# Three delays of 0.8 made 1.3 ahead of the weight products in an eight-pass graph kernel

## The chip, the cores and the metric

The kernel runs on one core of a Trainium2 chip. The metric is the device time of one execution in microseconds (us). A core has five engines that run side by side, each through its own queue in program order: TensorE (PE, matrix products; PEld are its weight loads), VectorE (DVE), ScalarE (ACT), GpSimd (POOL) and SyncE (SP, which here issues the loads from memory). An engine that needs another's result waits for a semaphore.

## The reference, cut to what matters

A graph of 3327 nodes with 64 features each has one adjacency matrix `adj`. Four residual layers follow one another, each on the layer norm of `x` cut at zero. Written out by its products with a 3327 x 3327 matrix, the work is eight passes:

```python
h = relu(layernorm(x))
# layer 0: two gated cells, each with m = adj @ h             -> passes 0, 1
# layer 1: w @ h, w = weights by rank among the non-zeros     -> pass 2
# layer 2, with w = adj * adj, three hops:                    -> passes 3, 4, 5
for W, b in ((W0, b0), (W1, b1), (W2, b2)):
    h = w @ h
    h = h @ W.T + b
# layer 3, two hops:                                          -> passes 6, 7
for k in range(2):
    agg = adj @ h
    h = tanh(concatenate([agg, h], axis=1) @ W[k])
x = x + h
```

"Pass k" below is the kernel's own index `k`. Pass 3 is the first hop of layer 2; passes 6 and 7 are the two hops of layer 3.

## The kernel before, in words

**Tiling.** The nodes are padded to 26 blocks of 128 and split into two halves of 13. Four chunks of blocks (`CH`, L52) hold 3, 3, 3 and 4 blocks of each half: chunks 0, 1 and 2 are 384 columns wide, chunk 3 is 512. Chunks 0 and 1 are group 0, chunks 2 and 3 are group 1. A tile is 128 source nodes against all the target columns of a group. In pass 7 chunk 1 is split in two: chunk 4 (256 columns) and chunk 5 (128 columns).

**Units.** A unit `(k, c, t)` adds to the sums of pass k and chunk c what tile t gives: in all passes but pass 2 four matmul instructions at L607 (two for each half of the nodes, since the type is f32). 26 units finish the sums of a chunk. `alone` and `joint` (L639, L655) write the list of units once; at the end of a stage the last 6 or 8 tiles are gone through for one chunk and then for the other, so that one chunk's sums are ready while TensorE works on the other's. `run` (L711) goes through the list and issues it.

**What happens between the units.** When a chunk's sums are complete, `propagate` calls `begin(c, after[k](...))` (L613). The `after_k` functions are generators: they issue a few instructions and then `yield` a number of microseconds. `spend(us)` (L374) is called after every unit with that unit's estimated TensorE time, 0.86 x width / 512 (L611, `STREAM_US`): 0.645 for 384 columns, 0.86 for 512, 0.43 for 256 and 0.215 for 128. It takes that from every waiting generator's number, and one that reaches zero or less goes on at once, ahead of the next unit. So a `yield` sets after how many units the next instructions stand in the queues. What is left over from a wait isn't carried to the next. At the end of the list the remaining generators are finished in order (L1045).

**After pass 3** (`after_3`, L973): `evacuate` (L750) copies the sums from PSUM into a work tile, with ScalarE (L753) for chunks 1 and 3 and VectorE (L755) for 0 and 2; then `yield`; then `dense_to_nodes` (L759) issues 4 products per block through `mm` (L307) on TensorE; then `yield 0.8`; then VectorE adds the bias (L980).

**After passes 6 and 7** (`after_6`, L999; `after_7`, L1011): `evacuate_stacked` (L823) copies one half of the sums with ScalarE (L824) and the other with VectorE (L825) into `both[c]`; then `yield`; then `stacked_to_nodes` (L767) issues the products with the weights, 8 instructions per block, the first 4 of a block with the half that ScalarE copied and the next 4 with VectorE's (L774); then ScalarE's tanh. In pass 6 a `yield 8.0` and transposes on VectorE follow (L803); in pass 7 a `yield 0.8`, the addition to x on VectorE (L1019) and the DMA of the output, which ScalarE's queue issues (L1021).

**PSUM.** Eight banks of 512 columns: four for sums, four for the rest, handed out by `take` and given back by `give` (L316, L329), first in, first out. In pass 7 chunk 5 takes two banks for its sums, one for each half (L585).

**Squares.** Passes 3 to 5 need the squares of the tiles. `prepare` (L444) squares a tile some units ahead, and `square` (L438) gives it to ScalarE (L440), or, where `(t.q + c) % 3` is 0 and no generator of a chunk is under way, to VectorE (L442).

Of the kernel before, what the change touches and what calls it, by code (L numbers as in the profile page):

```python
# [96 lines left out]
def kernel(  # L97
# [198 lines left out]
    def blocks(c):  # L296
        return CH[c][1] - CH[c][0]
# [31 lines left out]
    def give(i):  # L329
        released[i] = max(released) + 1  # L330
        (idle_sums if i < 4 else idle_temps).append(i)

    def nodes(c):

        return feat.tile([P, blocks(c), 2, D], F32, name=f"y{c}")

    def flat(t):
        return t.rearrange("p b s d -> p b (s d)")

    def groups(t):  # L340
        return t.rearrange("p b s d -> p (b s) d")

    def xchunk(c):
        return xs[:, CH[c][0]:CH[c][1]]
# [405 lines left out]
    def evacuate(acc, c, busy=False):  # L750
        m = work.tile([P, CWM], F32, name="t2")[:, :width(c)]
        if c % 2 or busy:
            nc.scalar.copy(m, acc[0][1][:, :width(c)])  # L753
        else:
            nc.vector.tensor_copy(m, acc[0][1][:, :width(c)])  # L755
        give(acc[0][0])
        return m

    def dense_to_nodes(ft, w, c):  # L759

        i, ps = take()
        v = view(ps, c)
        for b in range(blocks(c)):
            mm(v[:, b, :], ft[:, b * P:(b + 1) * P], bd[:, w - WL1, :])
        return i, v

    def stacked_to_nodes(c, w):  # L767

        i, ps = take()
        v = view(ps, c)  # L770
        for b in range(blocks(c)):
            for s in range(2):
                for n in range(2):
                    nc.tensor.matmul(v[upper(n), b, upper(s)], both[c][:, s, b * P + n * D:b * P + (n + 1) * D], w(s),  # L774
                                     start=True, stop=True)
        return i, v
# [19 lines left out]
    def transpose_on_vector(h, c):  # L796

        for s in range(2):
            to = both[c][:, s].rearrange("p (b q n) -> p b q n", q=4, n=32)
            for q in range(4):  # L800
                for f in range(2):
                    at = (1 - s) * D + f * 32
                    nc.vector.transpose(to[at:at + 32, :, q], h[q * 32:(q + 1) * 32, :, s, f * 32:(f + 1) * 32])  # L803
                if q % 2:
                    yield 1.5
# [17 lines left out]
    def evacuate_stacked(acc, c):  # L823
        nc.scalar.copy(both[c][upper(0), 0], acc[0][1][upper(0), :width(c)])  # L824
        nc.vector.tensor_copy(both[c][upper(1), 1], acc[1][1][upper(1), :width(c)])  # L825
        for i in {acc[0][0], acc[1][0]}:
            give(i)
# [144 lines left out]

    def after_3(c, acc):  # L973
        m = evacuate(acc, c)
        yield 0.8
        v = dense_to_nodes(m, WL2, c)
        yield 0.8
        yk = nodes(c)
        n = 2 * blocks(c)
        nc.vector.tensor_tensor(groups(yk), v[1].rearrange("p b (s d) -> p (b s) d", d=D),  # L980
                                brow[:, 0:1, :].to_broadcast([P, n, D]), ALU.add)
        give(v[0])
        y[4][c] = yk
# [15 lines left out]

    def after_6(c, acc):  # L1000
        evacuate_stacked(acc, c)
        yield 0.8
        v = stacked_to_nodes(c, lambda s: w3[:, 0, s])
        yk = nodes(c)
        nc.scalar.activation(flat(yk), v[1], AF.Tanh)
        give(v[0])
        y[7][c] = yk
        yield 8.0
        yield from transpose_on_vector(yk, c)

    def after_7(c, acc):  # L1011
        evacuate_stacked(acc, c)
        yield 0.8
        v = stacked_to_nodes(c, lambda s: w3[:, 1, s])
        t = work.tile([P, 4, 2, D], F32, name="t2")[:, :blocks(c)]
        nc.scalar.activation(flat(t), v[1], AF.Tanh)
        give(v[0])
        yield 0.8
        nc.vector.tensor_tensor(flat(xchunk(c)), flat(xchunk(c)), flat(t), ALU.add)  # L1019
        g0, g1 = CH[c]  # L1020
        nc.scalar.dma_start(out=out[:, g0:g1], in_=xs[:, g0:g1])  # L1021

    after[:] = [after_0, after_1, after_2, after_3, after_4, after_5, after_6, after_7]


# [60 lines left out]
```

## Time and profile before

| | |
|---|---|
| device time, three runs | 708.05, 708.03, 707.58 us, median 708.03 |
| the profiled execution's own time | 707.41 us |
| its span, first to last instruction | 705.5 us, at 0.999 of TensorE's full clock |
| TensorE busy | 680.6 us (96%) |
| VectorE busy / ScalarE busy | 351.7 us (50%) / 271.3 us (38%) |
| loads of the adjacency matrix | 199.46 MB on SP's queue, 76.1% of 16 DMA engines' span |

The times of one profiled execution are in us from the start of the span. In lines of the timeline the columns are start, length, engine, line, operation, tiles, shapes and count; in brackets stands the idle time of the engine before it, and what ended it. Matmuls overlap, so a line's length includes the last one's way through the array. The first slices up to about 80 us are passes 0 and 1 with the constants, the stretch to about 335 us is mostly pass 2, then come passes 3 to 5 up to about 560 us, and passes 6 and 7 to the end.

### The profile page before, as it was taken

What the parts mean: (1) busy time and instruction counts of PE and PEld (TensorE: products, weight loads), DVE (VectorE), ACT (ScalarE), POOL (GpSimd) and SP (SyncE); (2) the same over time, 40 slices, a digit from 0 to 9 for tenths busy, and PEclk for the clock granted to TensorE, in tenths of its full rate; (3) what the DMA queues carried; (4) which work ended last, traced back from release to release, by engine and by line L of the source; (5) the groups of instructions that cost most, each with busy time, mean ns of one, the idle gap of its engine ahead of it and who ended that gap; (6) DMA issues with size and microseconds to landing.
All of it is one profiled execution on the core that took longest, in us unless ns stands there. A gap on an engine that the chain in (4) does not pass through costs nothing.

```text
span 705.5 us, 12624 instructions
## 1 busy us (share of the span) xinstructions
PE 680.6 (96%) x5100; PEld 362.5 (51%) x5100; DVE 351.7 (50%) x747; ACT 271.3 (38%) x421; POOL 75.7 (11%) x114
## 2 busy tenths in 40 slices
PE   1999999999999999999999999999999999999997
PEld 1454666643545787677444444333344444344464
DVE  7566835633997889847533105425271565005101
ACT  1014100212136888888997206832166500000101
POOL 4300000002291233111100000000000000000000
PEclk9999999999999999999999999999999999999999
DMA  9999996089688952683799649963997399917991
GB/s 337 401 387 404 405 406 239 1 337 384 204 284 299 313 176 83 241 296 103 266 369 354 242 163 408 405 262 112 392 366 271 105 397 405 407 64 282 403 402 36
DMA packets 68549, 201.31 MB, mean 285 GB/s; under 512 B 7228, under 2 KB 8228, under 8 KB 68492
## 3 DMA queue, kind: packets, MB, share of 16 engines
q1 hardware_dynamic: 65596, 199.46, 76.1%
q8 instruction: 40, 0.66, 0.4%
q10 hardware_dynamic: 720, 0.85, 0.3%
q0 software_dynamic: 2176, 0.20, 0.2%
q14 instruction: 17, 0.14, 0.1%
HBM read 199.45 MB, written 0.85 MB: 284 GB/s over the span
## 4 chain that ended last, share of the span: by engine, by line
PE 84%; DVE 9%; ACT 4%; issue 1%; DMA 1%; SPq 0%; ACTq 0%; DVEq 0%
PE sum L607 70%; PE temp L307 5%; ACT adj L440 4%; DVE adj L466 3%; PE temp L542 2%; PE temp L876 2%; PE sum L307 1%; PE temp L774 1%; PE sum L876 1%; DVE e L521 1%; DMA bd<-in_weights 1%; DVE both L825 1%; DVE adj L901 1%; DVE st L842 0%; DVE t L836 0%
## 5 line engine op out<-in xcount | busy, mean ns | idle before, releaser
L607 PE MATMUL sum<-adj,y 128*64 128x384 f32 (+3 forms) x3016 | 533.6, 501 | 0.8 <-DVE y L849 0.6
L607 PEld LDWEIGHTS sum<-adj,y 128*64 128x64 f32 x3016 | 233.7, 137 | 246.3 <-issue 220.9
L440 ACT ACTIVATE adj<-adj 128x768 f32<-128x768 f32 (+1 forms) x175 | 143.6, 892 | 47.3 <-PE sum L607 24.6
L466 DVE TENSOR_SCALAR adj<-adj 128x768 bf16<-128x768 f32 (+3 forms) x208 | 114.7, 599 | 39.1 <-PE temp L542 31.1
L824 ACT COPY both<-sum 64x384 f32<-64x384 f32 (+3 forms) x17 | 8.1, 478 | 196.4 <-PE sum L607 196.3
L607 PE MATMUL sum<-e,both 128*64 128x384 bf16 (+1 forms) x624 | 78.4, 339 | 0.5 <-DVE e L521 0.4
L523 ACT ACTIVATE e<-temp,bitsb 128x384 int16<-128x384 f32 (+1 forms) x117 | 66.1, 606 | 15.0 <-PE temp L307 9.9
L825 DVE COPY both<-sum 64x384 f32<-64x384 f32 (+3 forms) x17 | 9.7, 568 | 113.6 <-ACT both L824 112.4
L442 DVE TENSOR_TENSOR adj<-adj 128x768 f32<-128x768 f32 (+1 forms) x33 | 31.5, 1003 | 52.2 <-DMA adj<-in_adjT 33.4
L307 PE MATMUL temp<-adj,tri 128*64 128x384 bf16 (+1 forms) x332 | 56.8, 341 | 0.5 <-DVE e L521 0.2
L845 POOL TENSOR_TENSOR st<-st,mhalf 128x6 f32<-128x6 f32 (+1 forms) x16 | 24.5, 1529 | 288.9 <-DVE st L843 288.9
L607 PEld LDWEIGHTS <-both 128*64 128x64 bf16 x624 | 46.5, 110 | 15.5 <-issue 2.2
L307 PEld LDWEIGHTS <-tri 128*64 128x64 bf16 x416 | 33.4, 110 | 15.3 <-issue 7.4
L521 DVE TENSOR_SCALAR e<-temp 128x384 int16<-128x384 f32 (+1 forms) x49 | 30.1, 617 | 21.1 <-ACT e L523 10.5
L471 POOL DMA_DIRECT2D adj<-totals x52 | 32.7, 630 | 51.5 <-PE temp L307 42.9
L803 DVE STREAM_TRANSPOSE both<-y 32x96 f32<-32x96 f32 (+1 forms) x128 | 35.6, 278 | 2.9
L542 PE MATMUL temp<-adj,behind 128*64 128x384 bf16 x208 | 30.3, 339 | 0.9 <-DVE adj L466 0.7
L819 DVE STREAM_TRANSPOSE y<-t 32x96 f32<-32x96 f32 (+1 forms) x64 | 17.8, 278 | 25.2 <-ACT t L810 24.3
L542 PEld LDWEIGHTS <-behind 128*64 128x64 bf16 x208 | 17.0, 110 | 17.6 <-issue 15.9
L755 DVE COPY t<-sum 128x384 f32<-128x384 f32 x6 | 3.3, 554 | 35.4 <-PE sum L607 35.4
L876 PE MATMUL temp<-both,cells 128*64 128x384 f32 (+1 forms) x68 | 17.7, 521 | 0.2 <-DVE both L825 0.2
L523 ACT ACTIVATE e<-sum,bitsb 128x384 int16<-128x384 f32 (+1 forms) x28 | 16.6, 599 | 2.5 <-PE sum L307 2.0
(132 smaller groups left out, 307.5 us busy)
## 6 DMA issues: line engine op xcount, KB each, us to landing
adj<-in_adjT SPq DMA_DIRECT2D x130, 768.0 KB, 8.5
adj<-in_adjT SPq DMA_DIRECT2D x104, 896.0 KB, 12.5
xs<-in_x SPq DMA_DIRECT2D x1, 640.0 KB
adj<-totals POOLq DMA_DIRECT2D x26, 3.0 KB, 5.3
adj<-totals POOLq DMA_DIRECT2D x26, 3.5 KB, 3.6
out<-xs ACTq DMA_DIRECT2D x2, 192.0 KB
out<-xs ACTq DMA_DIRECT2D x1, 256.0 KB
stage<-in_weights SPq DMA_DIRECT2D x2, 112.0 KB, 13.4
```

Of the source, the lines that this page charges most:

```text
L307: nc.tensor.matmul(out[hs], lhsT[:, hs], rhs, start=start, stop=stop)
L440: nc.scalar.activation(sq, v, AF.Square)
L442: nc.vector.tensor_tensor(sq, v, v, ALU.mult)
L466: nc.vector.tensor_scalar(t.mask.view[:rows, half], t.view()[:rows, half], 0.0, None, op0=ALU.not_equal)
L471: nc.gpsimd.dma_start(out=t.mask.view[P - 1:P], in_=totals[t.g][t.q:t.q + D + 1:D, :])
L521: nc.vector.tensor_scalar(wide[:, s], ps[:, :w], BITS, 0.0, op0=ALU.add, op1=ALU.max)
L523: nc.scalar.activation(wide[:, s], ps[:, :w], AF.Relu, bias=bitsb)
L542: nc.tensor.matmul(counts[c][1][s * D:(s + 1) * D, :w], behind[:, NQ - 1 - t.q:NQ - 1 - t.q + D], t.mask.view[:, s, t.cols(c)], start=firs ...
L607: nc.tensor.matmul(acc[h][1][h * D:(h + 1) * D, :w], yq[h], rhs[h], start=first and n == 0, stop=last and n == len(terms) - 1)
L803: nc.vector.transpose(to[at:at + 32, :, q], h[q * 32:(q + 1) * 32, :, s, f * 32:(f + 1) * 32])
L845: nc.gpsimd.tensor_tensor(st[:, 3, :n], st[:, 2, :n], mhalf[:, :n], ALU.pow)
L876: nc.tensor.matmul(ps[upper(1 - s), :w], cells[:, cell, s, g, :], both[c][:, s], start=True, stop=True)
```

## The change

Three numbers: the `yield` between the copy of the sums and the products with the weights, in `after_3`, `after_6` and `after_7`.

```diff
     def after_3(c, acc):
         m = evacuate(acc, c)
-        yield 0.8
+        yield 1.3
         v = dense_to_nodes(m, WL2, c)
         yield 0.8
...
     def after_6(c, acc):
         evacuate_stacked(acc, c)
-        yield 0.8
+        yield 1.3
         v = stacked_to_nodes(c, lambda s: w3[:, 0, s])
...
     def after_7(c, acc):
         evacuate_stacked(acc, c)
-        yield 0.8
+        yield 1.3
         v = stacked_to_nodes(c, lambda s: w3[:, 1, s])
```

No instruction is added or dropped. `after_5`, which has the same shape, keeps its 0.8.

## The prediction

> **What bounds the kernel now.** I read the page's first part, then the waits of TensorE, then the timeline around each of the 13 products that the edit concerns, last the chain that ended last.
>
> ```profile
> PE 680.6 (96%) x5100; PEld 362.5 (51%) x5100; DVE 351.7 (50%) x747; ACT 271.3 (38%) x421; POOL 75.7 (11%) x114
> ```
>
> TensorE bounds the kernel, so only time in which it stands still can be won. Its waits from 335 us to the end:
>
> ```profile
> PE temp L774 <- DVE both L825: 0.9, 4, 0.3
> PE temp L774 <- ACT both L824: 0.3, 1, 0.3
> PE temp L307 <- ACT t L753: 0.3, 1, 0.3
> ```
>
> With one of 0.6 us for a layer norm (L849) that is all of them: in passes 3 to 7 TensorE waits for copies of sums, and never for a DMA. The idle times understate the cost, because a matmul's modelled end covers part of the gap. I measure from start to start instead. A product block without a wait and one with it, both 24 instructions of pass 6:
>
> ```profile
> 578.71 0.87 PE L774 MATMUL temp<-w,both 128*64 128x64 f32 x24
> 579.41 3.07 PE L607 MATMUL sum<-adj,y 128*64 128x384 f32 x17
> ```
>
> ```profile
> 627.16 0.47 ACT L824 COPY both<-sum 64x384 f32<-64x384 f32 x1 [42.23 <-PE sum L607]
> 627.66 0.56 DVE L825 COPY both<-sum 64x384 f32<-64x384 f32 x1 [34.76 <-ACT both L824]
> ...
> 627.80 0.28 PE L774 MATMUL temp<-w,both 128*64 128x64 f32 x4
> ...
> 628.28 0.80 PE L774 MATMUL temp<-w,both 128*64 128x64 f32 x20 [0.19 <-DVE both L825]
> ...
> 628.91 2.32 PE L607 MATMUL sum<-adj,y 128*64 128x512 f32 x10
> ```
>
> The first takes 0.70 us to the next unit (578.71 to 579.41), the second 1.11: chunk 2 loses 0.41. The copies follow each other, ScalarE 0.22 us after the sums' last matmul (which ends 0.86, one unit, before 627.80), VectorE after ScalarE; 1.33 us after the sums the second half is there (628.27). One unit of 0.86 is too short for that, two (1.72) are enough.
>
> **What the skill says.** The Trainium skill, "PSUM — Partial Sum Buffer", section "PSUM bank collisions raise a hardware error", says that software must keep two engines apart on one bank and quadrant, readers too. The trace agrees and is stricter: VectorE's copy waits for ScalarE's although they read different partitions, except in chunk 5, whose halves lie in two banks (701.11 and 701.16). "TensorE: Matmul & The Clock Gate", section on the 16 sub-arrays, says that weight loads can be pulled ahead of running matmuls while ScalarE and VectorE are strictly first in, first out. The trace agrees: 0.14 us loads lie inside 0.32 us steps. "DMA: Bandwidth & Descriptors", section "Anatomy of one DMA", says that a DMA's semaphore wait is done on the issuing sequencer. The trace agrees: ScalarE's last tanh (702.38) stands behind an output DMA (701.94) that waits for an add.
>
> **The change part by part.** First, where each product goes. After the sums: chunks 0 and 1 of pass 3 and chunk 0 of pass 6, and chunk 3 of pass 3, are followed by 384-wide units; 2 x 0.645 = 1.29 is just short of 1.3, so 3 units instead of 2. Chunk 2 of passes 3, 6 and 7 is followed by 512-wide units: 2 instead of 1. Chunks 1 and 3 of pass 6 are followed by 384 and 512: 1.505, so 2 units before and after; they don't move. Chunk 3 of pass 7 is followed by 0.645, 0.43, 0.215 in turn: 4 units (1.935) instead of 2 (1.075). Chunk 0 of pass 7 by 0.43s: 4 instead of 2. Chunk 4 by six units of 0.215, together 1.29: it falls behind all of them, to the end. Chunk 5 is at the end anyway.
>
> Then, what each stall is worth. Unstalled, 12 products of pass 3 take 0.65 (407.36 to 408.01, 413.18 to 413.83), 16 take 0.87 (513.32 to 514.19, the like products of pass 5); of L774, 24 take 0.70 and 32 take 0.94 (636.42 to 637.36).
>
> Pass 3, chunks 0 and 1, pass 6, chunk 0: no stall, gain 0. The moved adds, tanh and transposes come one unit later; the next pass needs them ten and more units later, which hides them. Chunk 2 of pass 3: 0.67 instead of 0.65, gain 0.02.
>
> Pass 3, chunk 3:
>
> ```profile
> 364.54 0.57 ACT L753 COPY t<-sum 128x512 f32<-128x512 f32 x1
> ...
> 365.16 1.09 PE L307 MATMUL temp<-bd,t 128*64 128x128 f32 x16 [0.27 <-ACT t L753]
> ...
> 366.08 6.30 PE L607 MATMUL sum<-adj,y 128*64 128x384 f32 x38
> ```
>
> The copy is late behind ScalarE's squares. Weight loads come every 0.32, each at the start of the matmul before its own; the last two before the product, at 363.75 and 364.07, put its due time at 364.72. It starts at 365.16, and takes 0.92: 0.44 + 0.05 = 0.49 lost. A unit later it is due at 365.36, the copy is there at 365.15: gain 0.49. The unit that is pulled ahead of it needs a square that ended before the copy began (ScalarE's queue is in order), so it doesn't wait. One thing more moves: chunk 3's generator lives a unit longer, so one square (tile 20, chunk 1) goes to ScalarE (0.74 each, 24 in a row from 365.00) instead of VectorE. It would end at 368.79 and is used near 369.8; later ones have more. Cost 0, or 0.74 if that cover is gone.
>
> Pass 6, chunk 2: gain 0.41; the product is now due at 628.66, past 628.27. Pass 7, chunk 2: 656.91 to 658.08 is 1.17, gain 0.47; due at 657.77, VectorE done at 657.39.
>
> Pass 7, chunk 3:
>
> ```profile
> 664.97 0.69 DVE L825 COPY both<-sum 64x512 f32<-64x512 f32 x1 [5.60 <-ACT both L824]
> ...
> 665.16 0.28 PE L774 MATMUL temp<-w,both 128*64 128x64 f32 x4
> ...
> 665.72 1.03 PE L774 MATMUL temp<-w,both 128*64 128x64 f32 x28 [0.27 <-DVE both L825]
> ...
> 666.59 2.76 PE L607 MATMUL sum<-adj,y 128*64 128x128 f32 x24
> ```
>
> 1.43 instead of 0.94: 0.49 lost. But here another wait takes its place. The sums' banks are given back in the order chunk 2, chunk 3 of pass 6, chunk 2, chunk 3 of pass 7, and taken in that order by chunk 0, chunk 4 and twice by chunk 5. Chunk 5's second half therefore writes the very bank that VectorE is emptying until 665.66. Before, the product stood ahead of it and took the wait; now chunk 5's first unit comes at 665.16 and waits to about 665.71, between 0.44 (if two of its passes run first) and 0.55. Gain between +0.05 and -0.06; I take 0.
>
> Pass 7, the tail. Chunk 0: 696.14 to 697.25, gain 0.41 on TensorE. Now the product runs 697.00 to 697.70, and with two more units chunk 4's sums end at 698.56 (before 698.98). But tanh (697.92 to 698.41), the add (to 699.00) and the output DMA's issue (0.34, to 699.37) now all stand ahead of chunk 4's copy in the queues: the add comes two units after the product, exactly at the end of chunk 4's units. So ScalarE copies at 699.47 instead of 698.78 (before 699.20), VectorE from 699.86 to 700.29, chunk 4's product ends at 700.29 + 0.05 + 0.40 = 700.74, tanh 700.96 to 701.34, add to 701.80, DMA issue to 702.17, chunk 5's tanh at 702.27, add, last DMA issue at 702.90. Before it stood at 703.01. Gain 0.11, between -0.2 (0.05 more per hand-over, six of them) and 0.41.
>
> Loads: SP issues the last 24 of pass 7 between 636.6 and 676.9; at the 405 GB/s of the full slices 24 x 768 KB need 46.6 us, to about 683, and the last tile is used at 694. DMA doesn't take the gain.
>
> Sum: 0.02 + 0.49 + 0.41 + 0.47 + 0 + 0.11 = 1.50. The profiled execution would go from 707.41 (span 705.5 and 1.9 around it) to 705.91. It lies 0.62 under the median of the runs shown; from 708.03 I forecast 706.5.
>
> **The rivals.** *More*: chunk 5's unit isn't held by the bank (+0.49), and the tail keeps its 0.41 (+0.30): gain 2.29, 705.7. Against it: the order of the banks is fixed by the code. *Less*: the tail costs its bad end (-0.2) and one of the three stalls is only half gone (0.2): 1.50 - 0.31 - 0.2 = 1.0, 707.0. For it: the tail's hand-overs are all taken at their shortest. *Nothing*: the edit doesn't do what it says, the stalls return at the next unit, as the bank shows for chunk 3 of pass 7: 708.0. Against it: elsewhere no unit needs a bank just emptied. *Slower*: ScalarE's strict queue. If the squares have less than 0.74 us of slack at tile 20 (the chain passes through L440 from 336 to 364), the added square holds TensorE by 0.74 and chunk 3's 0.49 is not won, and in the tail the late copy costs 0.5: -(0.02 + 0.41 + 0.47) + 0.74 + 0.5 = +0.34, 708.4. It decides where TensorE would reach that unit before 368.8; I expect about 369.8.
>
> **How the numbers follow.** Forecast 0.50 (its own range 706.0 to 707.0), more 0.15, less 0.20, nothing 0.09, slower 0.06. The range takes in more and less: 705.6 to 707.4; nothing and slower, 0.15, stay out. About 0.2% (1.4 us) is what a measurement of this kernel can tell from no change. The forecast lies just beyond it: 0.35 of its 0.50 and all of "more" give faster 0.50; 0.05 of slower and some unseen wait give slower 0.06; same 0.44.
>
> **What would show it.** The products of chunk 2 (passes 6, 7) and of chunk 3 (pass 3) take 0.70 and 0.87 to the next unit, without a wait; chunk 5's first L607 waits for VectorE L825 by 0.4 to 0.6; the output DMA of chunk 0 is issued between tanh and chunk 4's copy; 25 squares stand in a row on ScalarE. I am wrong if TensorE waits for L440 near 369, or if the tail from chunk 0's last unit (695.28) to the last DMA issue is over 7.9 us.

## The result, and the profile after

| | before | after |
|---|---|---|
| device time, median of 11 runs | 708.03 us | 706.86 us |
| ratio, 95% interval | | 0.9981 (0.9973 to 0.9989) |
| profiled execution: span | 705.5 us | 703.7 us |

By the ratio the gain is 1.3 us of 708.03, between 0.8 and 1.9 (the two medians differ by 1.17); forecast were 1.5 (706.5). The interval lies wholly on the faster side, but it doesn't settle whether the gain is more or less than 0.2%.

Where in the profiled executions the time went is told by marks that both have: the start of a copy of sums. Of the 1.84 us between the spans, 0.40 had gone before the first edited place was reached (chunk 2's copy of pass 3 starts at 356.10 and 355.70). Up to there the programs are the same, so two executions differ by that much on their own. The rest, in us:

| from | to | before | after | difference | forecast |
|---|---|---|---|---|---|
| copy of chunk 2, pass 3 | copy of chunk 0, pass 3 | 50.19 | 49.67 | -0.52 | -0.51 |
| ... | copy of chunk 2, pass 6 | 220.87 | 220.88 | +0.01 | 0 |
| ... | copy of chunk 2, pass 7 | 29.16 | 28.75 | -0.41 | -0.41 |
| ... | copy of chunk 3, pass 7 | 8.04 | 7.57 | -0.47 | -0.47 |
| ... | copy of chunk 0, pass 7 | 31.14 | 31.24 | +0.10 | 0 |
| ... | issue of the last output DMA | 7.51 | 7.36 | -0.15 | -0.11 |
| together | | 346.91 | 345.47 | -1.44 | -1.50 |

The whole stretch, from the start of chunk 2's copy of pass 3 to the issue of the last output DMA, is the measure of the experiments below: all that the edit touches lies in it, and nothing of what differs at the start.

The first part of the page of the kernel after follows. The busy times are nearly those of before, and one instruction has gone from VectorE to ScalarE:

```profile
PE 679.8 (97%) x5100; PEld 372.9 (53%) x5100; DVE 350.1 (50%) x746; ACT 271.8 (39%) x422; POOL 80.0 (11%) x114
```

TensorE's waits from 335 us on (engine, line and tile, who was waited for: us in total, times, longest). The products L774 and L307 are gone from the list, and one wait is new, that of L607 for VectorE's copy (L825):

```profile
PE sum L607 <- DVE y L849: 0.6, 1, 0.6
PE sum L607 <- DVE both L825: 0.2, 1, 0.2
```

In the timeline of the kernel after at pass 6, chunk 2, VectorE's copy ends at 627.31. The 24 products begin at 627.75 and are one group; it is 0.69 us from their start to the next unit, where it was 1.11.

```profile
626.25 0.47 ACT L824 COPY both<-sum 64x384 f32<-64x384 f32 x1 [42.23 <-PE sum L607]
...
626.75 0.56 DVE L825 COPY both<-sum 64x384 f32<-64x384 f32 x1 [34.76 <-ACT both L824]
...
627.75 0.87 PE L774 MATMUL temp<-w,both 128*64 128x64 f32 x24
628.44 6.83 PE L607 MATMUL sum<-adj,y 128*64 128x512 f32 x32
```

At pass 3, chunk 3, it is 0.87 from the product to the next unit, without a wait. ScalarE's copy is as late as before, behind its squares, but the product now comes one unit later.

```profile
364.14 0.58 ACT L753 COPY t<-sum 128x512 f32<-128x512 f32 x1
...
364.94 1.04 PE L307 MATMUL temp<-bd,t 128*64 128x128 f32 x16
365.81 6.62 PE L607 MATMUL sum<-adj,y 128*64 128x384 f32 x40
```

And at pass 7, chunk 3, where the wait was forecast to move: chunk 5's first unit (128 columns) now waits for the end of VectorE's copy, and the products behind it don't. Of that unit one half of the nodes runs at once and the other waits; the weight loads (the last two lines) show the two halves 0.55 us apart, 663.38 and 663.93, far more than the 0.17 us for which TensorE stood idle.

```profile
663.18 0.69 DVE L825 COPY both<-sum 64x512 f32<-64x512 f32 x1 [4.74 <-ACT both L824]
...
663.93 1.08 PE L607 MATMUL sum<-adj,y 128*64 128x128 f32 x6 [0.17 <-DVE both L825]
664.63 1.13 PE L774 MATMUL temp<-w,both 128*64 128x64 f32 x29
...
663.38 0.14 PEld L607 LDWEIGHTS sum<-adj,y 128*64 128x64 f32 x1
663.93 0.20 PEld L607 LDWEIGHTS sum<-adj,y 128*64 128x64 f32 x4 [0.42 <-DVE both L825]
```

In the tail, ScalarE's output DMA of chunk 0 stands ahead of its copy of chunk 4. In the kernel before it did so too, but its issue ended 0.28 us before the copy began, and the copy waited for its sums:

```profile
698.58 0.34 ACTq L1021 DMA_DIRECT2D out<-xs  x1
699.20 0.37 ACT L824 COPY both<-sum 64x256 f32<-64x256 f32 x1 [1.24 <-PE sum L607]
```

In the kernel after the copy follows 0.04 us behind the DMA's issue, and what it waited for is the add (VectorE, L1019) for which that DMA waited (the last line holds the copies of chunks 4 and 5 together):

```profile
696.23 0.49 ACT L1016 ACTIVATE t<-temp 128x384 f32<-128x384 f32 x1 [1.95 <-PE temp L774]
697.35 0.34 ACTq L1021 DMA_DIRECT2D out<-xs  x1
697.73 0.76 ACT L824 COPY both<-sum 64x256 f32<-64x256 f32 x2 [1.00 <-DVE xs L1019]
```

### The profile page after: what moved, and what is told of

Its sections match the earlier page's. It is cut to its first block, busy times and chain, and to the rows that moved or that the text cites. A ratio compares the mean times of both kernels' runs of the same rounds, so it can differ in the third digit from the quotient of the medians.

```text
span 703.7 us, 12628 instructions
## 1 busy us (share of the span) xinstructions
PE 679.8 (97%) x5100; PEld 372.9 (53%) x5100; DVE 350.1 (50%) x746; ACT 271.8 (39%) x422; POOL 80.0 (11%) x114
## 4 chain that ended last, share of the span: by engine, by line
PE 91%; DVE 7%; issue 0%; ACT 0%; DMA 0%; POOL 0%; ACTq 0%; DVEq 0%; POOLq 0%
PE sum L607 77%; PE temp L307 5%; PE temp L542 2%; PE temp L876 2%; PE sum L307 1%; DVE adj L466 1%; PE temp L774 1%; PE sum L876 1%; DVE e L521 1%; DVE st L842 1%; DVE adj L901 1%; DVE t L836 1%; DVE y L841 0%; DVE st L834 0%; DMA xs<-in_x 0%
## 5 line engine op out<-in xcount | busy, mean ns | idle before, releaser
L607 PE MATMUL sum<-adj,y 128*64 128x384 f32 (+3 forms) x3016 | 534.5, 502 | 0.7 <-DVE y L849 0.6
L607 PEld LDWEIGHTS sum<-adj,y 128*64 128x64 f32 x3016 | 243.5, 137 | 237.3 <-issue 212.4
L440 ACT ACTIVATE adj<-adj 128x768 f32<-128x768 f32 (+1 forms) x176 | 144.2, 893 | 45.8 <-PE sum L607 21.9
L607 PE MATMUL sum<-e,both 128*64 128x384 bf16 (+1 forms) x624 | 78.5, 339 | 0.5 <-DVE e L521 0.5
L825 DVE COPY both<-sum 64x384 f32<-64x384 f32 (+3 forms) x17 | 9.6, 569 | 110.5 <-ACT both L824 110.5
L307 PE MATMUL temp<-adj,tri 128*64 128x384 bf16 (+1 forms) x332 | 56.8, 341 | 0.5 <-DVE e L521 0.2
L607 PEld LDWEIGHTS <-both 128*64 128x64 bf16 x624 | 46.6, 110 | 15.5 <-issue 2.2
L307 PEld LDWEIGHTS <-tri 128*64 128x64 bf16 x416 | 33.5, 110 | 15.3 <-issue 7.1
L564 POOL MEMSET adj<- 128x768 f32 (+1 forms) x2 | 1.9, 950 | 145.3 <-PE sum L607 145.3
```

The costliest lines, as they stand in the source:

```text
L307: nc.tensor.matmul(out[hs], lhsT[:, hs], rhs, start=start, stop=stop)
L440: nc.scalar.activation(sq, v, AF.Square)
L607: nc.tensor.matmul(acc[h][1][h * D:(h + 1) * D, :w], yq[h], rhs[h], start=first and n == 0, stop=last and n == len(terms) - 1)
```

## The experiments

**The theory:** each product that waited gains its own wait, and only that. Five products waited; the gains of two don't arrive, one held by a PSUM bank and one mostly by ScalarE's queue. **The rivals:** the added square on ScalarE takes part of the gain; or the delay counts in proportion, and not by whole units; or the waits come back elsewhere.

### One pass at a time

Three kernels have one of the three edits alone: the first in `after_3` (pass 3), the second in `after_6` (pass 6), the third in `after_7` (pass 7). The edited line is the same in each; the lines behind it show the three places (cut between them):

```diff
-        yield 0.8
+        yield 1.3
         v = dense_to_nodes(m, WL2, c)
...
-        yield 0.8
+        yield 1.3
         v = stacked_to_nodes(c, lambda s: w3[:, 0, s])
...
-        yield 0.8
+        yield 1.3
         v = stacked_to_nodes(c, lambda s: w3[:, 1, s])
```

Pass 3 alone:

> Only pass 3 has 1.3. Measure: the stretch from chunk 2's copy of the sums of pass 3 (VectorE L755 near 356) to the issue of the last output DMA (L1021); 346.91 us in the kernel before, 345.47 in the changed one, a difference of -1.44. My theory, that each product which waited gains its own wait and nothing else: -0.51 (0.02 at chunk 2, 0.49 at chunk 3), so 346.40, and chunks 2 and 3 of pass 7 wait as before. Rival, that the later place gives ScalarE an extra square which holds TensorE: -0.5 + 0.74, about +0.2. Rival, that the stalls return at the next unit: 0.

Pass 6 alone:

> Only pass 6 has 1.3. Stretch from L755 near 356 to the last output DMA: 346.91 before. My theory: only chunk 2's product gains, 0.41 to 0.42; chunk 0 moves for nothing, chunks 1 and 3 don't move: 346.49. Rival, stalls return elsewhere: 346.91.

Pass 7 alone:

> Only pass 7 has 1.3. Stretch: 346.91 before. My theory: chunk 2 gains 0.46, chunk 3 nothing (its wait goes to chunk 5's first unit, L607 waits for L825), chunk 0 gains 0.41 and gives 0.3 to 0.4 back behind the output DMA: 0.5 in all, 346.4. Rival, each product gains its wait: 0.46 + 0.49 + 0.41 = 1.36, 345.55.

Measured, from the copy to the last DMA: pass 3 alone 356.26 to 702.67, which is 346.41 (-0.50); pass 6 alone 356.71 to 703.22, 346.51 (-0.40); pass 7 alone 355.94 to 702.33, 346.39 (-0.52). They add up to -1.42, and the whole edit has -1.44: the parts are separate, and none comes back elsewhere. Pass 7, which had waits of 1.37 us at three products, gives only 0.52. Single runs of these kernels took 706.98, 707.63 and 706.74 us beside 707.69 for the kernel before; such single times can't tell parts of half a us apart, but the stretch can.

### 1.2 instead of 1.3

```diff
-        yield 1.3
+        yield 1.2
```

in all three places of the changed kernel.

> 1.2 instead of 1.3 in all three places. If whole units decide: 384-wide sites stay at 2 units, so chunk 3 of pass 3 keeps its wait (loses 0.49 of the gain); the two chunk 2 products still move (0.42 + 0.46); in pass 7 chunk 0's product stands after 3 units, its add and output DMA one unit further ahead of chunk 4's copy, and chunk 4's product ahead of chunk 5's copy, which I work out as 0.54 gained in the tail: -1.47 in all, 345.44, with L307 waiting 0.3 at chunk 3 of pass 3. If the delay itself decides in proportion (0.4 of 0.5): 0.8 x 1.44, at 345.76, with part of each wait left.

Measured: 357.55 to 703.18, 345.63 (-1.28). This lies between the two totals, so the single places have to decide. TensorE's waits from 335 us on:

```profile
PE temp L774 <- ACT both L824: 0.6, 1, 0.6
...
PE temp L307 <- ACT t L753: 0.3, 1, 0.3
PE sum L607 <- DVE both L825: 0.2, 1, 0.2
```

Chunk 3 of pass 3 (L307) waits as in the kernel before: two units of 0.645 are 1.29, so 1.2 leaves it where it was. The chunk 2 products don't wait at all. That is the mark of whole units: in proportion, a part of each wait would be left.

The total is 0.19 short of what I had worked out. Of this, 0.10 is lost at the bank, as in the changed kernel (31.24 us from chunk 3's copy to chunk 0's), and 0.04 in the tail; the other 0.05 is in the -1.47 itself, whose three terms come to 1.42. In the tail chunk 4's tanh came ahead of chunk 5's copy on ScalarE, which I had put earlier, and the last product waits for it (the 0.6 in the first line). Even so the tail, from chunk 0's copy to the last DMA, takes 7.01 us, against 7.51 in the kernel before and 7.36 in the changed one. Chunk 0's product stands one unit further ahead, so do its add and its DMA, and chunk 4's copy waits for its sums again:

```profile
699.27 0.34 ACTq L1021 DMA_DIRECT2D out<-xs  x1
699.65 0.36 ACT L824 COPY both<-sum 64x256 f32<-64x256 f32 x1 [1.00 <-PE sum L607]
```

So in the tail 1.2 is 0.35 us better than 1.3. A kernel with 1.3 in passes 3 and 6 and 1.2 in pass 7 was not run.

### Another bank for chunk 5

```diff
-            sums[k, c] = [take(sums=True) for _ in range(2 if k == 7 and c == PARTS[1] else 1)]
+            sums[k, c] = [take(sums=True)]
+            if k == 7 and c == PARTS[1]:
+                sums[k, c].append(take(either=False))
```

on top of the changed kernel. The line numbers behind this edit are 2 higher.

> The changed kernel, with chunk 5's second bank in pass 7 taken from the banks that aren't used for sums, instead of the one that VectorE is emptying. My theory, that the bank holds chunk 5's first unit: this wait goes and the 0.49 of chunk 3's product is won: stretch 345.47 - 0.49 = 344.98, and no L607 waits for L825. Rival, that chunk 5's unit waits for something else there (its tile, ScalarE): no change, 345.47. Against the kernel before: -1.9 us, ratio 0.9973.

Measured: 355.88 to 700.76, 344.88, which is 0.59 less than the changed kernel, all of it from chunk 3's copy to chunk 0's (31.24 became 30.65); time ratio to the kernel before 0.9972 (0.9963 to 0.9982). Of TensorE's waits from 335 us on one is left:

```profile
PE sum L609 <- DVE y L851: 0.6, 1, 0.6
```

In the timeline at chunk 3 of pass 7 VectorE's copy runs from 663.36 to 664.05, and chunk 5's first unit, whose second half now goes to `temp`, no longer waits for it.

```profile
663.56 0.27 PE L609 MATMUL temp<-adj,y 128*64 128x128 f32 x1
663.66 0.27 PE L609 MATMUL sum<-adj,y 128*64 128x128 f32 x1
663.67 0.27 PE L609 MATMUL temp<-adj,y 128*64 128x128 f32 x1
663.77 0.81 PE L609 MATMUL sum<-adj,y 128*64 128x384 f32 x4
664.41 1.10 PE L776 MATMUL temp<-w,both 128*64 128x64 f32 x32
```

So it was the bank: a wait for a tile or for ScalarE, the rival, would have stayed in place.

### The squares on ScalarE

```diff
-        if turn % 3 or any(ch in tasks or (2, ch) in sums for ch in range(NC)):
+        if turn % 3 or any(ch in tasks or (2, ch) in sums for ch in range(NC)) or (3, GROUPS[0][0]) in sums:
```

on top of the changed kernel.

> The changed kernel, with all squares of passes 3 and 4 for group 0 on ScalarE while chunk 0's sums of pass 3 are open: some 13 more than the one that the change moved, 0.74 us each. My theory, that ScalarE has a lead over TensorE there: stretch unchanged at 345.47 (within 0.1), and no wait of TensorE for L440. Rival, that ScalarE's queue is near the path: TensorE waits for L440 and the stretch grows by 0.7 us or more.

Measured: 357.61 to 703.07, 345.46, against 345.47, and TensorE's list has no wait for L440. ScalarE squared 189 times where the changed kernel does 176, VectorE 19 times where it does 32:

```profile
L440 ACT ACTIVATE adj<-adj 128x768 f32<-128x768 f32 (+1 forms) x189 | 153.5, 887 | 44.2 <-PE sum L607 21.9 <-ACT adj L440 10.8 <-DMA adj<-in_adjT 9.7
```

(the columns are the count, busy us and mean ns, and the idle time before them with what ended it). Thirteen more squares cost nothing, so the one that the edit moved cost nothing either: ScalarE runs ahead of TensorE there. In the kernel before, the chain of waits from 330 to 420 us passed through L440 for 28% of its length. That didn't mean that the squares bound this stretch: the chain followed ScalarE's row of squares back from one late copy, that of chunk 3.

### The tail as before

```diff
-        yield 1.3
+        yield 1.3 if c in GROUPS[1] else 0.8
         v = stacked_to_nodes(c, lambda s: w3[:, 1, s])
```

on top of the changed kernel.

> The changed kernel, with 0.8 as before in pass 7 for chunks 0, 4 and 5; chunks 2 and 3 keep 1.3. My theory: chunk 0's 0.41 is lost again, and what the queue gave back is not given back: 0.0 to 0.1 slower, stretch 345.5. Rival, that the tail kept the gain of chunk 0's product: 0.4 slower, 345.9.

Measured: 357.62 to 703.24, 345.62, 0.15 more than the changed kernel. This is a little over the 0.1 expected, and well under 0.4: of the 0.41 that chunk 0's product won, 0.15 arrives at the end.

### The output DMAs on SP's queue

```diff
-        nc.scalar.dma_start(out=out[:, g0:g1], in_=xs[:, g0:g1])
+        nc.sync.dma_start(out=out[:, g0:g1], in_=xs[:, g0:g1])
```

on the changed kernel, on the changed kernel with the other bank, and on the kernel before.

On the changed kernel:

> The changed kernel, with the output DMAs issued from SP's queue, which has nothing left to do after the loads, instead of ScalarE's. My theory, that chunk 0's DMA, waiting for its add, holds chunk 4's copy on ScalarE: the copy comes 0.6 to 0.7 us earlier, and the last tanh no longer stands behind the DMA of chunk 4: the last DMA is issued 1.2 us earlier in the stretch: 344.3. Rival, that the copies and products of chunks 4 and 5 set the tail anyway: -0.3 at most. Against the kernel before: -2.6 us, ratio 0.9963.

With the other bank too:

> The changed kernel with both: another bank for chunk 5, and the output DMAs from SP's queue. If they are separate: -0.49 - 1.2, stretch 343.8, against the kernel before -3.1 us, ratio 0.9956. If they overlap, no better than the better of the two.

On the kernel before:

> The kernel before (0.8 everywhere) with the output DMAs from SP's queue. My theory: chunk 4's copy doesn't stand behind a DMA there, only the last tanh does, so 0.5 us: stretch 346.4. Rival, that ScalarE's queue costs the same in both kernels: 1.2 us, 345.7. It tells how much of the changed kernel's gain the tail gave back through the queue.

Measured: 344.80, 345.08 and 348.07; ratios to the kernel before 0.997 (0.996 to 0.9981), 0.9977 (0.9968 to 0.9986) and 1.0022 (1.0016 to 1.0029). All three missed, the last by 1.7 us and in its sign. The tail itself did as the theory says: from chunk 0's copy to the last DMA it takes 6.36 us instead of 7.36 in the first two, and 7.06 instead of 7.51 on the kernel before. What was lost lies ahead of it, from chunk 3's copy to chunk 0's: 31.57 instead of 31.24, 31.86 instead of 30.65 and 32.75 instead of 31.14. SP's timeline in the last of the three kernels shows why:

```profile
668.21 0.37 SPq L1021 DMA_DIRECT2D out<-xs  x1
668.67 14.54 SPq L405 DMA_DIRECT2D adj<-in_adjT  x10
```

and TensorE's:

```profile
666.64 28.59 PE L607 MATMUL sum<-adj,y 128*64 128x128 f32 x252
696.26 1.73 PE L607 MATMUL sum<-adj,y 128*64 128x384 f32 x12 [1.03 <-DMA adj<-in_adjT]
```

SP's queue is empty only for the last three output DMAs. Those of chunks 2 and 3 are issued while the last loads still stand in it; each waits for its add, and the loads behind it wait too. The last load is issued by 683.2 instead of 676.9 and lands at 696.2 instead of 690.6, and TensorE waits for its tile. In the second kernel TensorE waits likewise (1.0 us). In the first its list shows no wait for a DMA; there it is a weight load that waited for the last tile, which landed at 693.1:

```profile
693.16 0.20 PEld L607 LDWEIGHTS sum<-adj,y 128*64 128x64 f32 x4 [0.77 <-DMA adj<-in_adjT]
```

I had looked at the end of the queue and not at each place where the edit put an instruction. So the edit was made again, with only the tail's three DMAs on SP:

```diff
-        nc.scalar.dma_start(out=out[:, g0:g1], in_=xs[:, g0:g1])
+        (nc.scalar if c in GROUPS[1] else nc.sync).dma_start(out=out[:, g0:g1], in_=xs[:, g0:g1])
```

on the changed kernel, without the other bank:

> The changed kernel, with only the last three output DMAs (chunks 0, 4 and 5) on SP's queue; those of chunks 2 and 3 stay on ScalarE's. My theory now: the loads are no longer held behind an output DMA, TensorE doesn't wait for a tile, and the tail keeps the 1.0 us that the earlier version won from chunk 0's copy to the last DMA (7.36 to 6.37): stretch 345.47 - 0.99 = 344.48; against the kernel before -2.4 us, ratio 0.9966. Rival, that the loads are late for another reason: a wait for a DMA near 695 stays, and the stretch is 344.8.

With the other bank:

> The same with chunk 5's second bank from the other pool. If the two are separate: 344.88 - 0.99 = 343.89; against the kernel before -3.0 us, ratio 0.9958. Rival, that TensorE's earlier arrival meets the last loads: a wait for a DMA near 694, and 344.2 to 344.5.

Measured: 355.45 to 699.95, 344.50, and 355.99 to 699.89, 343.90; neither has a wait for a DMA in TensorE's list. ScalarE's tail in the first of the two:

```profile
695.98 0.49 ACT L1016 ACTIVATE t<-temp 128x384 f32<-128x384 f32 x1 [1.95 <-PE temp L774]
696.85 0.37 ACT L824 COPY both<-sum 64x256 f32<-64x256 f32 x1 [0.37 <-PE sum L607]
```

Chunk 4's copy waits for its sums (PE) and starts 0.87 us after the tanh did; in the changed kernel it waited for the add, behind which the DMA stood, and started 1.50 after. That is the 0.63 which the queue took. Ratios to the kernel before: 0.9964 (0.995 to 0.9977) and 0.9967 (0.9954 to 0.9979). Both intervals lie well under 1, so both beat the kernel before. By the stretch the second is the shortest of all, 3.0 us under the kernel before and 1.6 under the changed one; the times don't tell the two apart, and their intervals overlap with the changed kernel's (0.9973 to 0.9989).

## Why the prediction was right

**The units.** That 1.3 moves a product by one unit or two, and chunks 1 and 3 of pass 6 not at all, came from the code's 1.29 and 1.505. The run with 1.2 showed the same rule from the other side.

**The three plain gains** (pass 3 chunk 3, pass 6 chunk 2, pass 7 chunk 2) were 0.49, 0.41 and 0.47 in the forecast and are 0.50, 0.41 and 0.47 by the marks. The idle times of the waits list, 0.3, 0.2 and 0.2, would have given about half. Measuring from start to start, against a group that doesn't wait, was the step that sized them.

**The bank.** The forecast was between +0.05 and -0.06, taken as 0; by the marks 0.10 is lost. The mechanism was right, as the run with another bank shows. The wait was sized a little too small: without it the place takes 30.65 us, so the product does win its 0.49 against the 31.14 before, and the wait costs 0.59 where 0.44 to 0.55 were forecast. The second half's 0.55 explains most of it; the last 0.04 stay open.

**The tail.** Forecast was 0.11, measured 0.15. The steps between hold as well: chunk 4's copy was to start 3.97 us after chunk 0's, and starts 3.92 after (693.81 to 697.73). That ScalarE's queue took the rest is shown by the kernels with the tail's DMAs on SP. There chunk 4's copy starts 3.70 us after chunk 0's with 0.8 and 3.29 with 1.3, so the 0.41 arrives in full; with the DMAs on ScalarE it starts 3.70 after with 0.8, but 3.92 with 1.3.

**The square.** The prediction named the lead that would cover the added square, and nothing was lost; the thirteen more squares show that the lead is long. The rival "slower" falls with it. (26 squares stand in a row on ScalarE, not the 25 forecast, but only one more is done there in all.)

**The loads.** That the loads wouldn't take the gain was right, but the margin was given too large. I had the last tile land at about 683 against a use at 694. By the trace of the kernel before, the last load is issued at 676.4 and lands 14.2 us later, at 690.6, and the unit that uses its tile comes near 694.6: the margin was about 4 us, not 11. The rate that I took, 405 GB/s, holds from 646 to 686 us (404), but from 636.6 to 646 it is 242 and from 686 to 691 it is 196. In the kernel before with its DMAs on SP the last load lands 5.6 us later, 1.6 more than the margin, and 1.6 us is what it lost from chunk 3's copy to chunk 0's.

The sum was -1.50, against -1.44 by the marks and -1.3 (-1.9 to -0.8) by the runs. Its two misses, 0.10 lost at the bank and 0.04 more won in the tail, cancel in part and are small beside it. It stood so near 0.2% that even odds on "faster by more than that" were as much as could be said, and the runs still don't decide it.

## What to carry to other kernels

A wait ahead of an instruction, on an engine that works its queue in order, costs the difference to a like group without the wait, measured from start to start. Moving the instruction back by one unit of other work wins just that, if what takes its place has no wait of its own: look up which buffer that one writes and who is still reading it. More delay isn't always better: near the end of a kernel look at every queue that the moved step issues to, for there a DMA that waits for its data holds the copy behind it. And before putting DMAs into an idle queue, find each of their places in it, not only the last.

## What the runs showed that I had not expected

Two executions of nearly the same program differ by 0.4 us and more up to the first edited place: chunk 2's copy of pass 3 starts between 355.45 and 357.62 over the fourteen profiles. The stretch after it repeats far more closely: the three parts of the edit add up to the whole within 0.02, and the kernel with thirteen more squares on ScalarE differs by 0.01. So the marks in one profile resolved parts of half a us, where eleven timed runs of each kernel left an interval of 1.1 us.
